# Ready steps by age with a credit for a bank, and attention masks as quarter products, in a planned four-layer transformer kernel

## The chip, the cores and the metric

The kernel runs on one core of one Trainium2 chip. The metric is the device time of one execution in microseconds, the median of three runs. A profile of one further execution, taken by the hardware profiler, stands beside it.

## The reference, cut to what matters

Four diffusion-transformer layers run one after the other over x of 16 x 256 x 256 (16 examples, 256 positions, width 256, 16 heads of 16), all in float32. The part that the change touches is the first layer's self-attention, which has a mask:

```python
def _attn(q, k, v, mask):
    scale = 1.0 / np.sqrt(HD)
    s = jnp.einsum('bqhd,bkhd->bhqk', q, k) * scale
    s = jnp.where(mask, s, jnp.finfo(s.dtype).min)
    a = jax.nn.softmax(s, axis=-1)
    return jnp.einsum('bhqk,bkhd->bqhd', a, v)
...
x_norm = _ln(x, norm1_w) * (1 + sc_msa) + sh_msa
q1, k1, v1 = qkv(x_norm[:, :n])
...
self_out = _attn(q, k, v, attn_mask[None, None]).reshape(b, s, d) @ attn_out_W
x = x + g_msa * self_out
xc = _ln(x, normc_w) * (1 + sc_x) + sh_x
...
cross = _attn(qc, kc, vc, cond_kv_mask[:, None, None, :]).reshape(b, s, d) @ co_W
x = x + g_x * cross
xm = _ln(x, norm2_w) * (1 + sc_mlp) + sh_mlp
h = jax.nn.gelu(xm @ mlp_W1 + mlp_b1, approximate=True)
return x + g_mlp * (h @ mlp_W2 + mlp_b2)
```

The mask of the self-attention is one table of 256 x 256 for all examples and heads. The second layer is a cross-attention alone (77 keys), the third has self-attention, cross-attention and an MLP without masks, and the fourth the same with rotated queries and keys.

## The kernel before, in words

**The work.** The activations stay in SBUF (`x_sb`). Six stretches follow each other: the attentions of layer 0 (names a for self, ac for cross), its MLP (b), the attentions of layers 1 and 2 (cx, c, cc), an MLP (d), those of layer 3 (e, ec), and the last MLP (f). Each attention of one example is a chain of steps: norm, projections (L591, L643, L763), first scores (L804 for self, L816 for cross) with queries along the partitions, from which VectorE takes each row's maximum (L830, L834, L838); these maxima go through DRAM into the extra rows of the queries; second scores (L898) with keys along the partitions, so that ScalarE's exponential (L912) gives what the product with the values needs (L921); a turn of the result on VectorE (L930), the reciprocal of the sums (L937, called the division here), the multiplication on GpSimd (L943), a turn back (L947), and the output projection with the residual (L968).

**Tiles of the array.** A head has 16 values, padded to a group of 32 rows of the array. Four groups of rows work side by side, each into its own bank of PSUM. A step of scores fills two banks (`rp` picks rows 0 and 32, or 64 and 96), and the planner puts two such steps together so that all four row groups are in use. The value products (L921) use four groups of columns in the same way.

**The mask in layer 0.** In the first scores of examples 0 and 1 (`by_pe`) the mask is a product with the identity in bf16 (L795), over the whole array, 512 columns into one bank; for the other 14 examples VectorE adds it while it takes the maximum (L830, one instruction and a short read-out for each half bank). In the second scores every bank gets its mask by such a product (L891): two products of the whole array for each step, ahead of the row-tiled scores L898, which add onto them. The masks `mb` and `mbT` (its transpose) are made at the start by `masks_in` and lie in a tile that a context buffer lends.

**What sets the order.** Nothing is scheduled by the hardware or a compiler here. The class `Order` collects all steps with an engine, an estimated duration, the steps they depend on and the buffers they take or use (`Hold`: PSUM banks "b", of which there are 8, and others such as `ts`, two, `oT`, two, `kq`, five). `solve` plays the steps through with those durations and so writes down one fixed order; each engine then executes its instructions in it. A buffer is given back when all its users are done. When an engine is free, `solve` sorts the steps that are ready (L178 to L179): on TensorE by priority, which rises with the example and the stage; on SP by `first`, then priority; on all other engines by `first`, then steps that hold a PSUM bank ahead of all others, then by the time at which they became ready. On ScalarE every step of the attentions and MLPs holds a bank, on GpSimd none does. On VectorE both kinds occur: reductions, L930, L616, the rotations (L655, L658) and the gated residuals hold one; the norm statistics (L466, L467), the division L937 and the turn back L947 don't. The estimate of a step of second scores is 2 x 0.432 us, and 0.48 more with a mask; that of a masked reduction is 0.95 us.

Of the kernel before, what the change touches and what calls it, by code (L numbers as in the profile page):

```python
# [16 lines left out]
B, N, D, H, HD, LC, FF = 16, 256, 256, 16, 16, 77, 1024  # L17
P = 128
NT = N // P
NC = D // P  # L20
NF = FF // P
CT = B * LC
# [51 lines left out]
class Order:  # L74
# [2 lines left out]
    LAG = 0.13  # L77
    TURN = {"row": 0.2, "col": 0.13}
    PATIENCE = 2.0
    PER_MB = 2.7  # L80
    FREE = ("b", "kq", "v")

# [20 lines left out]
    def solve(self):  # L103
# [66 lines left out]
        while n_done < len(self.tasks):  # L170
            progress = True
            while progress:
                progress = False
                for eng in list(waiting):
                    if eng != "NO" and free.get(eng, 0.0) > now + 1e-9:
                        continue
                    cand = [t for t in waiting[eng] if t.ready <= now + 1e-9]
                    cand.sort(key=lambda t: (t.prio, t.no) if eng == "PE" else (not t.first, t.prio, t.no) if eng == "SP" else  # L178
                              (not t.first, not any(h.tag == "b" for h in t.held), t.ready, t.prio, t.no))  # L179
                    cand = [t for t in cand if room(t)]  # L180
                    if cand:
                        ts = choose(cand) if eng == "PE" else [cand[0]]
                        if ts is not None:
                            begin(ts)
                            progress = True
            nxt = [e[0] for e in events[:1]]
            nxt += [t.ready for ts in waiting.values() for t in ts if t.ready > now + 1e-9]
            nxt += [t.since + self.PATIENCE for t in waiting.get("PE", ())
                    if t.since is not None and t.since + self.PATIENCE > now + 1e-9]
            assert nxt, "no step can start"  # L190
            now = min(nxt)
            while events and events[0][0] <= now + 1e-9:
                _, _, t = heapq.heappop(events)
                n_done += 1
                for h in t.held:
                    h.users -= 1
                    if not h.users and h.tag in loose:
                        loose[h.tag].append(h.no)
                    elif not h.users:
                        done_no[h.tag].add(h.no)  # L200
                        while ring[h.tag] in done_no[h.tag]:
                            done_no[h.tag].discard(ring[h.tag])
                            ring[h.tag] += 1
                for u in t.outs:
                    u.left -= 1
                    u.ready = max(u.ready, t.end + (self.LAG if u.eng != t.eng else 0.0))
                    if not u.left:
                        waiting.setdefault(u.eng, []).append(u)
# [4 lines left out]
def pixart_kernel(ctx: ExitStack, tc: tile.TileContext, x, cond_t, ctx_in, mask_c, mask_s, tables, vecs, rows,  # L213
                  mod0, mod1, mod2, mod3, wa, wb, wc, wd, we, wf, out):
    nc = tc.nc
    PSUM = bass.MemoryType.PSUM
    BF16 = mybir.dt.bfloat16
# [12 lines left out]
    ps = ctx.enter_context(tc.tile_pool(name="ps", bufs=1, space=PSUM))  # L230
# [3 lines left out]
    def psum(h, *dims):  # L234

        t = banks[h.no]
        return t.rearrange("p (a b) -> p a b", a=dims[0]) if dims else t
# [4 lines left out]
    identb = const.tile([P, P], BF16, name="identb")  # L242
# [14 lines left out]
    h_mask = Hold("ctx")  # L257
# [26 lines left out]
    add = od.add  # L284
    MM = 0.432
# [43 lines left out]
    t = add("PE", 0.4, rows_turn, take=[h_rt], prio=200)  # L329
# [360 lines left out]
    def attention(b, name, n, wv, wkeys, h_w, w_t, eps, mod, half, biases, masked, pre_add, gate, prio, ctxs=None,  # L690
# [177 lines left out]
        for g in range(NC):  # L868
            u5, h_av, h_so = {}, Hold("b"), Hold("ts")
            for kc in range(nk):  # L870
                h_e, ex = Hold("ec"), []

                def open_e(g=g, kc=kc):
                    if g == 0 and kc == 0:
                        s["oT"] = work.tile([P, NC, N], F32, tag="oT", bufs=CAPS["oT"], name=f"oT_{nm}")
                    for r in range(4):
                        s["e", g, kc, r] = work.tile([P, 2, N], F32, tag="e", bufs=4 * CAPS["ec"],
                                                     name=f"e_{nm}_{g}{kc}{r}")
                t_e = add("NO", 0.0, open_e, deps=[qx_t, v_t, barrier], take=[h_e] if g or kc else [h_e, h_ot],
                          prio=prio, line=("e", (nm, g, kc)))  # L880
                for rp in (1, 0):
                    hs = [Hold("b"), Hold("b")]
                    u = {}

                    def begin(g=g, kc=kc, rp=rp, u=u, hs=hs):
                        lists = []
                        for i in range(2):
                            r = 2 * rp + i
                            ps = u[i] = psum(hs[i])
                            if self_ and masked:  # L890
                                nc.tensor.matmul(ps.rearrange("p (s k) -> p s k", k=N), lhsT=identb,  # L891
                                                 rhs=mbT[:, kc, :].unsqueeze(1).to_broadcast([P, 2, N]),
                                                 start=True, stop=False)
                        for i in range(2):
                            r = 2 * rp + i
                            R = slice(32 * r, 32 * r + 32)
                            lists.append([
                                (lambda ps=u[i], R=R, q=q: nc.tensor.matmul(  # L898
                                    ps[0:rows_n, q * N:(q + 1) * N],
                                    lhsT=s["kz"][R, q, g, kc * P:kc * P + rows_n], rhs=s["qx"][R, q, g, :],  # L900
                                    start=not (self_ and masked), stop=not (self_ and masked) or q == 1))
                                for q in range(2)])
                        return lists
                    a = add("PE", 2 * MM, begin, more=0.48 if self_ and masked else 0.0,
                            deps=[t_e, k_t, *(mask_ts[self_][1] if masked else [])], take=hs, use=[h_kq, *h_masks], prio=prio, rp=rp, kind="e")
                    for i in range(2):
                        def exp(g=g, kc=kc, r=2 * rp + i, i=i, u=u):
                            e = s["e", g, kc, r][0:rows_n].rearrange("p s q -> p (s q)")
                            if masked and not self_:
                                nc.scalar.activation(e, u[i][0:rows_n], AF.Exp, bias=kbT[0:rows_n, b:b + 1])  # L910
                            else:
                                nc.scalar.activation(e, u[i][0:rows_n], AF.Exp)  # L912
                        ex.append(add("ACT", 0.6, exp, deps=[a], use=[hs[i], h_e], prio=prio))
                exps += ex

                def values(g=g, kc=kc, u5=u5, h_av=h_av):
                    if kc == 0:
                        u5["p"] = psum(h_av, 2)
                    for q in range(2):
                        for r in range(4):  # L920
                            nc.tensor.matmul(u5["p"][32 * r:32 * r + 32, 1 - q, :],  # L921
                                             lhsT=s["v"][0:rows_n, kc, 8 * g + 2 * r + 1 - q, :],
                                             rhs=s["e", g, kc, r][0:rows_n, q, :],
                                             start=(kc == 0 and q == 0), stop=(kc == nk - 1 and q == 1))
                a_av = add("PE", 2 * MM, values, deps=ex, take=[] if kc else [h_av],
                           use=[h_v, h_e] + ([h_av] if kc else []), prio=prio, kind="col", line=("av", (nm, g, kc)))
# [114 lines left out]

    mask_t = work.tile([P, NC, CT], F32, tag="ctxT", bufs=CAPS["ctx"], name="ctxT_masks")
    add("NO", 0.0, lambda: None, take=[h_mask], prio=-9)
    mask_b = mask_t.rearrange("p c n -> p (c n)")[:, 0:1152].bitcast(BF16)
    mb, mbT = (mask_b[:, i * 512:(i + 1) * 512].rearrange("p (t n) -> p t n", n=N) for i in range(2))
    junk = const.tile([P, N], F32, name="junk")
    kbm = mask_b[:, 1024:1024 + CT].rearrange("p (b n) -> p b n", n=LC)

    def load_x(b, prio, deps=()):
        def run():  # L1050
# [22 lines left out]
    def masks_in(prio):  # L1073
# [15 lines left out]

        def take():  # L1090
            nc.vector.tensor_copy(mbT, psum(hb, NT))
        t = add("SP", ISSUE, load, take=[hg], prio=prio, mb=0.07, lat=2.2)
        t = t1 = add("DVE", 1.2, floats, deps=[t], take=[ht], use=[hg, h_mask], prio=prio)
        t = add("PE", 4 * TR, turn, deps=[t], take=[hb], use=[ht], prio=prio)
        return t1, add("DVE", 0.5, take, deps=[t], use=[hb, h_mask], prio=prio)

    def key_masks_in(prio):
        u, hg, hb = {}, Hold("gb"), Hold("b")
# [244 lines left out]
```

## Time and profile before

| what | value |
|---|---|
| median of three runs | 2724.95 us (2724.75 to 2725.81) |
| the profiled execution, its own time | 2725.6 us |
| its span, first to last instruction | 2723.8 us |
| mean granted TensorE clock | 0.989 |
| TensorE busy | 2672.4 us (98%) |
| VectorE, ScalarE, GpSimd busy | 1543.9, 1238.8, 1064.8 us |
| chain that ended last | TensorE 92%, VectorE 3%, GpSimd 3% |
| masks of the second scores, L891 | 256 products, 376/379/634 ns (shortest, median, longest) |
| masked reductions, L830 | 448 at 423 ns, 189.4 us busy |

How to read it: PE is TensorE's products and PEld its loads of weights, DVE is VectorE, ACT ScalarE, POOL GpSimd, SP the engine that issues transfers. A matmul's end is modelled, and its recorded duration includes the way through the array, so products that follow each other overlap in the records: the distance of starts says what one costs. A busy TensorE is therefore not a TensorE at its peak, and the number of matmuls that pass in a stretch has to be compared. A product in fp32 stands in the trace as two matmuls. "Idle before, with a releaser" is how long an engine stood still before an instruction and what ended that.

### The profile page before, as it was taken

The page shows a single profiled execution, that of the slowest core. Times are in us where ns is not written, and L with a number is a line of the kernel's source. Part 1 is how long each engine was busy: PE and PEld are TensorE (multiplying, and loading weights), DVE is VectorE, ACT ScalarE, POOL GpSimd, SP SyncE. Part 2 cuts the span into 40 slices and gives each one's busy share as a digit, 9 for nine tenths or more (in the row PEclk, how much of TensorE's full clock was granted, in tenths as well). Part 3 has the DMA queues.
Part 4 walks back from the last instruction along what each step waited for, and adds up shares of the span by engine and source line. Part 5 has one row for each costly group of instructions (what it writes and reads, how often), then busy time and mean ns, then how long its engine had stood idle before and what let it go on. Part 6 is the DMA issues. An engine that isn't in the chain of part 4 may idle for free.

```text
span 2723.8 us, 55987 instructions
## 1 busy us (share of the span) xinstructions
PE 2672.4 (98%) x21888; PEld 1896.5 (70%) x21888; DVE 1543.9 (57%) x4377; ACT 1238.8 (45%) x2495; POOL 1064.8 (39%) x1413
## 2 busy tenths in 40 slices
PE   8999999999999999999999999999999999999999
PEld 5554555666888767666666676888766666666888
DVE  6787686566231267767776675110688876784110
ACT  2442444565332356555555554332445555554322
POOL 4322332455453435233334554433333323554321
PEclk9997999999999999999999999999999999999999
DMA  4000000011210010010000002000000000000000
GB/s 143 11 9 10 6 7 6 18 27 56 82 46 20 9 30 6 11 31 16 19 15 13 5 13 77 20 20 12 17 4 4 4 4 5 4 21 23 20 20 20
DMA packets 53569, 60.23 MB, mean 22 GB/s; under 512 B 19592, under 2 KB 38264, under 8 KB 52536
## 3 DMA queue, kind: packets, MB, share of 16 engines
q1 hardware_dynamic: 53304, 56.65, 7.1%
q8 instruction: 172, 2.82, 0.4%
q14 instruction: 93, 0.76, 0.1%
HBM read 50.44 MB, written 6.19 MB: 21 GB/s over the span
## 4 chain that ended last, share of the span: by engine, by line
PE 92%; DVE 3%; POOL 3%; issue 1%; ACT 1%; DMA 1%; DVEq 0%; POOLq 0%; ACTq 0%; SPq 0%
PE bank L968 19%; PE bank L898 13%; PE bank L1011 12%; PE bank L921 11%; PE bank L804 7%; PE bank L591 7%; PE bank L643 6%; PE bank L763 5%; PE bank L502 3%; PE bank L891 2%; PE bank L816 2%; PE bank L683 2%; DVE junk L830 1%; PE bank L387 1%; PE bank L578 0%
## 5 line engine op out<-in xcount | busy, mean ns | idle before, releaser
L898 PE MATMUL bank<-kq 32*128 32x256 f32 (+1 forms) x5120 | 596.6, 395 | 4.4 <-DMA kq<-mrow 3.6
L898 PEld LDWEIGHTS bank<-kq 32*128 32x128 f32 (+1 forms) x5120 | 349.3, 168 | 176.7 <-issue 120.5
L804 PE MATMUL bank<-kq 32*128 32x512 f32 x1536 | 408.9, 647 | 1.7 <-DVE kq L616 1.6
L912 ACT ACTIVATE e_a<-bank 128x512 f32<-128x512 f32 x256 | 136.8, 598 | 203.3 <-PE bank L804 120.6
L830 DVE CUSTOM_DVE_ANT_0 junk<-bank,ctxT_masks 128x256 f32<-128x256 f32 x448 | 189.4, 423 | 61.3 <-PE bank L804 28.9
L912 ACT ACTIVATE e_e<-bank 128x512 f32<-128x512 f32 x256 | 136.6, 599 | 145.4 <-PE bank L804 120.3
L834 DVE TENSOR_REDUCE mx_c<-bank 128x2 f32<-128x512 f32 x256 | 160.1, 682 | 36.5 <-PE bank L804 36.0
L834 DVE TENSOR_REDUCE mx_e<-bank 128x2 f32<-128x512 f32 x256 | 161.7, 683 | 31.2 <-PE bank L804 30.1
L912 ACT ACTIVATE e_c<-bank 128x512 f32<-128x512 f32 x256 | 134.6, 602 | 98.0 <-PE bank L804 70.1
L974 DVE TENSOR_TENSOR x_sb<-x_sb,bank 128x512 f32<-128x512 f32 x80 | 54.8, 684 | 210.4 <-PE bank L968 205.9
L816 PE MATMUL bank<-kq 32*128 32x154 f32 x2048 | 167.2, 309 | 0.2
L804 PEld LDWEIGHTS bank<-kq 32*128 32x128 f32 x1536 | 131.7, 186 | 37.4 <-DVE mx_a L830 11.5
L816 PEld LDWEIGHTS bank<-kq 32*128 32x128 f32 x2048 | 130.1, 185 | 14.9 <-issue 6.7
L1016 ACT ACTIVATE h_d<-bank,vec 128x256 f32<-128x256 f32 x128 | 53.7, 471 | 156.0 <-PE bank L1011 105.8
L1016 ACT ACTIVATE h_f<-bank,vec 128x256 f32<-128x256 f32 x128 | 53.7, 471 | 153.3 <-PE bank L1011 133.3
L1016 ACT ACTIVATE h_b<-bank,vec 128x256 f32<-128x256 f32 x128 | 53.6, 471 | 146.3 <-PE bank L1011 118.6
L1011 PE MATMUL bank<-xT_b,kq 128*128 128x256 f32 x512 | 113.8, 379 | 0.0
L1011 PE MATMUL bank<-xT_d,kq 128*128 128x256 f32 x512 | 113.6, 380 | 0.0
L1011 PE MATMUL bank<-xT_f,kq 128*128 128x256 f32 x512 | 113.3, 379 | 0.0
L968 PE MATMUL bank<-kq,h_b 128*128 128x256 f32 x512 | 113.2, 379 | 0.0
L968 PE MATMUL bank<-kq,h_d 128*128 128x256 f32 x512 | 113.2, 379 | 0.0
L968 PE MATMUL bank<-kq,h_f 128*128 128x256 f32 x512 | 113.2, 379 | 0.0
(335 smaller groups left out, 5777.2 us busy)
## 6 DMA issues: line engine op xcount, KB each, us to landing
kq<-in_mod_dram SPq DMA_DIRECT2D x10, 512.0 KB
cin<-in_ctx_in_dram SPq DMA_DIRECT2D x36, 128.0 KB
x_sb<-in_x_dram SPq DMA_DIRECT2D x16, 256.0 KB
gb_b<-gate_g0m SPq DMA_DIRECT2D x16, 256.0 KB
gb_c<-gate_g2a SPq DMA_DIRECT2D x16, 256.0 KB
gb_d<-gate_g2m SPq DMA_DIRECT2D x16, 256.0 KB
out_dram<-x_sb SPq DMA_DIRECT2D x16, 256.0 KB
kq<-mrow SPq DMA_DIRECT2D x224, 16.0 KB
```

The costliest lines, as they stand in the source:

```text
L591: nc.tensor.matmul(dst[:, g, :], lhsT=w[:, k, g * P:(g + 1) * P], rhs=xT[:, k, :], start=(k == 0), stop=(k == NC - 1))
L643: nc.tensor.matmul(u["p"][0:r, at:at + D], lhsT=xT()[:, k, t * P:t * P + r], rhs=w()[:, k, :], start=(k == 0), stop=(k == NC - 1))
L804: ls.append(lambda ps=ps, R=R, keys=keys: nc.tensor.matmul(ps.rearrange("p (s k) -> p s k", k=N), lhsT=s["qx"][R, 0, g, t * P:(t + 1) * P] ...
L816: ls.append(lambda ps=ps, R=R, keys=keys, tt=tt: nc.tensor.matmul(ps[:, 2 * tt * n:2 * (tt + 1) * n].rearrange("p (s k) -> p s k", k=n), l ...
L830: nc.vector.tensor_tensor_reduce(junk, u[i][:, i2 * N:(i2 + 1) * N], mb[:, t, :], -1.0, 3.0e38, ALU.add, ALU.min, m[:, i2, g, t:t + 1])
L834: nc.vector.tensor_reduce(m[:, :, g, t], u[i].rearrange("p (s k) -> p s k", k=N), AX.X, ALU.max, negate=True)
L898: (lambda ps=u[i], R=R, q=q: nc.tensor.matmul(ps[0:rows_n, q * N:(q + 1) * N], lhsT=s["kz"][R, q, g, kc * P:kc * P + rows_n], rhs=s["qx"][ ...
L912: nc.scalar.activation(e, u[i][0:rows_n], AF.Exp)
L921: nc.tensor.matmul(u5["p"][32 * r:32 * r + 32, 1 - q, :], lhsT=s["v"][0:rows_n, kc, 8 * g + 2 * r + 1 - q, :], rhs=s["e", g, kc, r][0:rows ...
L968: nc.tensor.matmul(u["p"][:, t, :], lhsT=lhsT(k, t), rhs=w()[:, k, :], start=(k == 0), stop=(k == nk - 1))
L1011: nc.tensor.matmul(u["p"][:, j, :], lhsT=wv["w1"][:, k, f * P:(f + 1) * P], rhs=s["xT"][:, k, :], start=(k == 0), stop=(k == NC - 1))
L1016: nc.scalar.activation(s["h", i][:, j, :], u["p"][:, j, :], func, bias=vcol(b1, 2 * i + j))
```

## The change

Two edits.

In the planner, the sort key of VectorE, ScalarE and GpSimd no longer puts every step that holds a bank first. Steps are taken by the time at which they became ready, and one that holds a bank counts as 3.0 us (`FAVOUR`) older than it is.

In the second scores of layer 0 the mask of a bank is no longer one product of the whole array. Each bank's product is cut in two halves of keys, 64 rows and 64 columns of the identity, and a step's four quarters are arranged so that they use the four quarters of the array: bank 0 takes keys 0 to 63 by rows 0 to 63 and keys 64 to 127 by rows 64 to 127; bank 1 takes keys 0 to 63 by rows 64 to 127 and keys 64 to 127 by rows 0 to 63. For bank 1 the mask therefore has to lie with its two halves of partitions swapped: `mbR`, a third tile of masks, is made at the start by two more copies out of PSUM. The planner's cost of the masks goes from 0.48 to 0.26 us a step, that of the step that makes the masks from 0.5 to 1.4.

```diff
+    FAVOUR = 3.0
...
-                              (not t.first, not any(h.tag == "b" for h in t.held), t.ready, t.prio, t.no))
+                              (not t.first, t.ready - self.FAVOUR * any(h.tag == "b" for h in t.held), t.prio, t.no))
...
-                            ps = u[i] = psum(hs[i])
-                            if self_ and masked:
-                                nc.tensor.matmul(ps.rearrange("p (s k) -> p s k", k=N), lhsT=identb,
-                                                 rhs=mbT[:, kc, :].unsqueeze(1).to_broadcast([P, 2, N]),
+                            u[i] = psum(hs[i])
+                        for j in range(2):
+                            for i in range(2 if self_ and masked else 0):
+
+                                K, M = slice(64 * (i ^ j), 64 * (i ^ j) + 64), slice(64 * j, 64 * j + 64)
+                                nc.tensor.matmul(u[i][M].rearrange("p (s k) -> p s k", k=N), lhsT=identb[K, K],
+                                                 rhs=(mbR if i else mbT)[K, kc, :].unsqueeze(1).to_broadcast([64, 2, N]),
                                                  start=True, stop=False)
...
-                    a = add("PE", 2 * MM, begin, more=0.48 if self_ and masked else 0.0,
+                    a = add("PE", 2 * MM, begin, more=0.26 if self_ and masked else 0.0,
...
-    mask_b = mask_t.rearrange("p c n -> p (c n)")[:, 0:1152].bitcast(BF16)
+    mask_b = mask_t.rearrange("p c n -> p (c n)")[:, 0:1408].bitcast(BF16)
...
-    kbm = mask_b[:, 1024:1024 + CT].rearrange("p (b n) -> p b n", n=LC)
+    mbR = mask_b[:, 1024:1536].rearrange("p (t n) -> p t n", n=N)
+    kbm = mask_b[:, 1536:1536 + CT].rearrange("p (b n) -> p b n", n=LC)
...
             nc.vector.tensor_copy(mbT, psum(hb, NT))
+            for i in range(2):
+                nc.vector.tensor_copy(mbR[64 - 64 * i:P - 64 * i], psum(hb, NT)[64 * i:64 * i + 64])
...
-        return t1, add("DVE", 0.5, take, deps=[t], use=[hb, h_mask], prio=prio)
+        return t1, add("DVE", 1.4, take, deps=[t], use=[hb, h_mask], prio=prio)
```

## The prediction

> **What bounds the kernel now.** I read the page's busy shares first, then the busy time by stretches of 50 us, then the waits and the timeline of the stretch that stood out, last the mask product's own records. TensorE is the bound:
>
> ```profile
> PE 2672.4 (98%) x21888; PEld 1896.5 (70%) x21888; DVE 1543.9 (57%) x4377; ACT 1238.8 (45%) x2495; POOL 1064.8 (39%) x1413
> ```
>
> So a gain is had only where TensorE works less or where its "busy" is hollow. Busy time by stretch (columns: stretch, length, then busy us and instructions of PE, PEld, DVE, ACT, POOL, then granted clock, DMA share, GB/s), layer 0's self-attention:
>
> ```profile
> 150.00:200.00 50.00, 50.00 (x411) 28.54 (x409) 42.12 (x174) 21.18 (x39) 13.15 (x16) 1.00 0.04 9
> 200.00:250.00 50.00, 48.68 (x251) 24.99 (x252) 43.30 (x193) 10.28 (x20) 6.68 (x8) 0.79 0.03 7
> 250.00:300.00 50.00, 45.20 (x367) 24.97 (x368) 23.30 (x86) 20.52 (x40) 16.76 (x23) 0.87 0.04 10
> 350.00:400.00 50.00, 50.00 (x423) 29.66 (x425) 40.42 (x161) 21.39 (x40) 17.39 (x22) 1.00 0.03 9
> ```
>
> All four claim a nearly full TensorE, yet 200 to 300 passes 618 matmuls where its neighbours pass about 418 per 50 us, 836 per 100: 218 are missing, 26 us at their rate, and the clock falls to 0.79. The timeline there (start, duration, what, idle before):
>
> ```profile
> 230.97 21.18 PE L804 MATMUL bank<-kq 32*128 32x512 f32 x44
> ...
> 257.50 0.23 DVE L937 RECIPROCAL rec_a<-ts_a 128x8 f32<-128x8 f32 x2
> ...
> 257.74 0.76 POOL L943 TENSOR_TENSOR od_a<-ts_a,rec_a 128x128 f32<-128x128 f32 x2 [28.50 <-DVE rec_a L937]
> 257.97 0.67 DVE L930 STREAM_TRANSPOSE ts_a<-bank 128x512 f32<-128x512 f32 x1
> 258.10 2.92 PE L968 MATMUL bank<-w_a,oT_a 128*128 128x256 f32 x6 [4.79 <-DVE oT_a L947]
> ```
>
> The turn L930 before this one stood at 214.5 (0.67 us); its division L937 starts at 257.50, 42 us late. It holds no bank, so on VectorE every ready reduction (L830) was put before it. Undivided tiles keep both `ts` buffers, so the next turn (257.97), the residual (258.10) and new second scores wait too. TensorE is left with first scores alone, one bank per reduction: 44 passes, 22 banks, in 21.2 us.
>
> **What the Trainium skill says.** "TensorE: Matmul & The Clock Gate", Part 3: products on different tiles of the array run together, "MM_dur + (ntile−1)×4ns". The trace agrees for rows and for columns apart: L898's records on other rows start 6 to 7 ns apart, so do L921's on other columns, and the next round 209 to 216 ns later; rows and columns at once, as in the change, it doesn't show. "TensorEngine Tiling (Array Packing)": by its Key Properties a change of tiling mode drains the array, by its Restrictions column tiling switches the fast weight load off. The drain is in the trace: mask product to scores takes 309 ns, mask product to mask product 216 to 226, so 93 ns (309 - 216) a change. Its Gotcha 1 says that row tiles cannot write one bank at the same time; "PSUM — Partial Sum Buffer", on bank collisions, puts the limit at bank and quadrant, and the quarters of one bank lie in other quadrants. Nothing in the trace settles this.
>
> **The change, part by part.** The sum is made against the profiled execution, 2725.6 us (span 2723.8, 1.8 around it); the median of the runs is 2724.95, 0.65 below, which I take off at the end.
>
> ```profile
> L891 PEld LDWEIGHTS <-identb x256: 95/98/151, 53.2 to 501.0; 128*128 128x128 bf16 x128
> L891 PE MATMUL bank<-ctxT_masks,identb x256: 376/379/634, 53.4 to 501.2; 128*128 128x512 bf16 x128
> ```
> ```profile
> 340.21 0.60 PE L891 MATMUL bank<-ctxT_masks,identb 128*128 128x512 bf16 x2
> 340.74 0.19 PEld L898 LDWEIGHTS bank<-kq 32*128 32x128 f32 x2 [0.42 <-issue]
> ```
>
> (1) Masks by quarters. A step of two banks now takes 0.535 us from its first mask product to its scores (226 + 309 ns; above, 340.21 to 340.74). There are 256 products in 128 steps. After: four quarters, 512 columns each. If they run together: one product of 216 ns, three starts 7 ns apart (21), the drain of 93, and a load that nothing hides. A first load of 128 fp32 columns lengthens its product by 104 ns (478 against 374), of 32 columns by 24 (403 against 379): 0.8 ns a column, so some 52 ns for 64 columns without the fast load. Sum 0.382, saved 0.153. Where two such steps stand together the second pair's loads hide, saved about 0.19 a step. I take 0.16: 128 x 0.16 = **-20.5 us**. Best end: a whole product saved, 128 x 0.216 = -27.6. Worst end: all four one after another, (4 x 226 - 2 x 226) x 128 = +58. TensorE is the bound here, so the saving is on the path as far as VectorE follows, term (4).
>
> (2) More changes of mode. In the order of the instructions, layer 0 passes 465 changes of tiling before and 518 after: mask products on the whole array could follow projections without one, quarters cannot. 53 x 0.093 = **+5 us**.
>
> (3) Age in place of banks first. In VectorE's order the most instructions between a turn L930 and its division falls from 163 to 30, the longest run of reductions from 64 to 32. After the opening, where no second scores exist yet, TensorE's longest run of first scores in layer 0 falls from 36 to 10. So this stall goes. Its size: the 22 banks alone took 21.2 us; in a full group (340.74 to 341.81) four banks take 1.07, so 22 take 5.9: 15.3 lost. The wait before L968 5, the waits for the rotated queries before 231 some 5, half clock on the way out some 3: 28, and 26 by the counted matmuls. I take **-28 us** (25 to 31). TensorE's groups are as many in both orders (layer 0: 197 and 196; last attention: 194 and 194); in the middle one 259 became 262, 3 x 1.0 = **+3 us**, between 0 and 5. ScalarE's steps all hold banks and GpSimd's none, so their rule stays in effect; SP's and TensorE's are untouched. Outside layer 0 the new rule only moves VectorE steps within slack: from 950 to 1650 VectorE is busy 481 of 700 us, from 1915 to 2480 442 of 565.
>
> (4) What is late next: VectorE. Never idle, it reads 43.3 of 50 (200 to 250), 0.87. From 50 to 500 it is busy 322.8, so it needs 371 us. TensorE would leave 450 - 28 - 20.5 = 402: VectorE at 92%. From 150 to 200 it ran at 42.1/43.3 = 97% with TensorE undisturbed, but the order is fixed from costs that put a masked reduction at 0.95 where the trace has 1.04 (241.76 to 242.80), so it will come late and hold banks. I give **+10 us**, from 0 to 16.
>
> (5) Two more copies of half a mask tile (L1097, L1098 of the new file), at most 0.74 each by L616's row for a whole tile, before the first L891 at 53 us; VectorE is busy 36 of the first 50 us, which hides them: 0, or +1.5 without that cover. Nothing is added to a queue of DMAs.
>
> Sum: -20.5 + 5 - 28 + 3 + 10 = **-30.5 us**: 2695.1 on the profiled scale, **2694** on the median's. Its own range: low ends -27.6 + 5 - 31 + 0 + 0 = -54, high ends -19.5 + 5 - 25 + 3 + 16 = -20: 2671 to 2705.
>
> **The rivals.**
> *VectorE takes the place of the bound.* Half of what TensorE is given back, (28 + 20.5)/2, is lost to banks that come late: -24 + 5 + 3 = -16, 2709. For it: the 92% above, and the waits for `mx_a` before L804. Against it: 97% without harm.
> *The quarters don't do what they say*: the pair on one bank runs after the pair before it. Two rounds cost as much as now plus the bare load (53 - 10) x 128 = +5.5; VectorE is then pressed less (+5): -28 + 5.5 + 5 + 3 + 5 = -9.5, 2715. For it: Gotcha 1. Against it: the quadrants differ.
> *Slower*: the quarters run one by one, loads included. +58 - 28 + 5 + 3 = +38, 2763. It decides from the point where a step of four quarters takes over 0.7 us to its scores, since 128 x (0.7 - 0.535) = 21 eats what the order's terms leave (28 - 5 - 3). For it: no product of this trace uses part of the rows and part of the columns. Against it: rows and columns each run together.
>
> **Numbers.** Forecast 0.60, VectorE 0.20, two rounds 0.12, one by one 0.08. The range reaches from the forecast's low end to the two rounds: 2671 to 2715, about 0.8 of the cases. A measurement of this kernel can tell some 0.2%, 5.4 us: the first three are faster by more, except a part of the two rounds and of VectorE's case (0.05), so faster 0.87, within 0.05, slower 0.08.
>
> **What would show it.** In the changed profile: 512 quarter products whose starts lie under 60 ns apart within a step, and some 0.38 us from the first to the scores (0.54: two rounds; over 0.7: one by one). No stretch of layer 0 with a clock of 0.8, the first MLP's products beginning some 34 us earlier, none of it from later layers; GpSimd's longest wait for L937 in layer 0 far below 28.5 us. VectorE at or above 41 of 50 us there; if waits of L804 and L898's loads for reductions grow beyond 10 us, VectorE's rival holds. Wrong would be a new stall of the same kind in a later attention, or a step's gain that VectorE eats whole.

## The result, and the profile after

The changed kernel takes 2685.03 us (median of four runs, 2683.71 to 2687.25), the kernel before 2724.85: a ratio of 0.9856, 95% interval 0.9838 to 0.9873. The forecast was 2694 with a range of 2671 to 2715, so the time lies inside, 9 us below the forecast.

The page of the changed kernel, busy times:

```profile
PE 2635.8 (98%) x22144; PEld 1887.2 (70%) x22144; DVE 1542.2 (57%) x4379; ACT 1240.1 (46%) x2495; POOL 1065.7 (40%) x1413
```

TensorE is as full as before with 37 us less in it. Busy time by stretches of 50 us (stretch, length, PE, PEld, DVE, ACT, POOL, granted clock, DMA share, GB/s), the same place in layer 0 as before:

```profile
150.00:200.00 50.00, 49.78 (x472) 29.12 (x474) 41.43 (x169) 23.03 (x43) 17.34 (x22) 1.00 0.03 9
200.00:250.00 50.00, 50.00 (x480) 31.17 (x468) 41.81 (x172) 23.93 (x46) 17.30 (x22) 1.00 0.04 9
250.00:300.00 50.00, 49.78 (x468) 29.12 (x464) 41.33 (x170) 22.59 (x42) 17.34 (x22) 1.00 0.03 9
```

These stretches now pass some 470 matmuls each, part of them short quarters, at the full clock; the hole of 251 at 0.79 is gone, and VectorE is at 41 to 42 of 50. The longest time from a turn to the division of its result in layer 0 (L934 to L941 in the changed kernel's numbering, L930 to L937 before) fell from 43.0 to 7.8 us, and GpSimd's longest wait for a division from 28.5 to 13.7. The quarter products, by their records and in the timeline:

```profile
L895 PEld LDWEIGHTS <-identb x512: 102/103/106, 54.5 to 457.8; 64*64 64x64 bf16 x171
L895 PE MATMUL bank<-ctxT_masks,identb x512: 372/400/400, 54.5 to 458.0; 64*64 64x512 bf16 x171
```
```profile
340.79 0.41 PE L895 MATMUL bank<-ctxT_masks,identb 64*64 64x512 bf16 x4
341.13 0.19 PEld L902 LDWEIGHTS bank<-kq 32*128 32x128 f32 x2 [0.23 <-issue]
```

The four stand in one line because they start 3 to 4 ns apart; 0.34 us later the scores begin, where two whole products took 0.535. The last mask product stands at 458.0, before at 501.2.

Where the time went, by the start of the first product of each stretch (us of the span, from the records of the two profiles):

```
                     before   after
layer 0 attentions    683.2   641.9   -41.3
first MLP             239.1   239.0
layers 1, 2           761.6   760.7    -0.9
second MLP            232.0   232.0
last attentions       575.0   576.0    +1.0
last MLP              233.0   233.1
```

The whole gain is in layer 0's attentions.

### The profile page after: what moved, and what is told of

Read it like the earlier page. It is cut to its first block, busy times and chain, and to the rows that moved or that the text cites. A ratio compares the mean times of both kernels' runs of the same rounds, so it can differ in the third digit from the quotient of the medians.

```text
span 2682.7 us, 56475 instructions
## 1 busy us (share of the span) xinstructions
PE 2635.8 (98%) x22144; PEld 1887.2 (70%) x22144; DVE 1542.2 (57%) x4379; ACT 1240.1 (46%) x2495; POOL 1065.7 (40%) x1413
## 4 chain that ended last, share of the span: by engine, by line
PE 92%; DVE 3%; POOL 2%; ACT 1%; issue 1%; DMA 1%; DVEq 0%; ACTq 0%; POOLq 0%; SPq 0%
PE bank L972 20%; PE bank L902 13%; PE bank L1015 12%; PE bank L925 11%; PE bank L805 7%; PE bank L592 7%; PE bank L644 6%; PE bank L764 5%; PE bank L503 3%; PE bank L817 2%; PE bank L684 2%; PE bank L895 2%; PE bank L388 1%; PE bank L579 0%; ACT e_ac L914 0%
## 5 line engine op out<-in xcount | busy, mean ns | idle before, releaser
L902 PE MATMUL bank<-kq 32*128 32x256 f32 (+1 forms) x5120 | 606.2, 396 | 2.9 <-DMA kq<-mrow 2.5
L902 PEld LDWEIGHTS bank<-kq 32*128 32x128 f32 (+1 forms) x5120 | 354.3, 168 | 158.4 <-issue 108.2
L805 PE MATMUL bank<-kq 32*128 32x512 f32 x1536 | 411.1, 638 | 1.9 <-DVE kq L617 1.8
L805 PEld LDWEIGHTS bank<-kq 32*128 32x128 f32 x1536 | 127.4, 184 | 25.2 <-issue 8.1
```

What stands on the lines that cost most here:

```text
L805: ls.append(lambda ps=ps, R=R, keys=keys: nc.tensor.matmul(ps.rearrange("p (s k) -> p s k", k=N), lhsT=s["qx"][R, 0, g, t * P:(t + 1) * P] ...
L902: (lambda ps=u[i], R=R, q=q: nc.tensor.matmul(ps[0:rows_n, q * N:(q + 1) * N], lhsT=s["kz"][R, q, g, kc * P:kc * P + rows_n], rhs=s["qx"][ ...
```

## The experiments

Each was timed in four to six runs beside the kernel before, and a bracket after a ratio is its 95% interval; "layer 0" is the first stretch of the table above in the run's own profile. The kernel before had medians of 2724.8 to 2726.9 beside them. Two profiles of one layer 0 order differ by up to 3.7 us (the changed kernel and favour_e0), so single layer 0 lengths are not read finer than that. Medians are compared with the changed kernel's 2685.03, which was measured at another time; differences of some 2 us, the range of the kernel before, are not read.

**masks_only**: the quarters with the old sort key.

```diff
-  (not t.first, t.ready - self.FAVOUR * any(h.tag == "b" for h in t.held), t.prio, t.no))
+  (not t.first, not any(h.tag == "b" for h in t.held), t.ready, t.prio, t.no))
```

> The quarter products with the sort key of before (banks first). Theory that two separate gains add up (masks about 25 us, since a step falls from 0.535 to 0.340 us 128 times; order the rest): about 2700 us, with a stall of the old kind (first scores alone, a division L937 that comes tens of us late) still in layer 0. Rival, VectorE takes the place of the bound without the new order: the steps are as short, but the stalls grow and the time stays above 2712 us.

Measured 2738.53 us, ratio 1.0051 (1.0039 to 1.0063): slower than before; layer 0 694.1. The steps are as short as in the changed kernel (0.340 us). The stretches and the timeline of this run:

```profile
150.00:200.00 50.00, 49.83 (x357) 23.25 (x350) 42.36 (x186) 14.63 (x26) 3.74 (x3) 0.90 0.04 10
...
400.00:450.00 50.00, 44.09 (x278) 22.53 (x280) 33.31 (x134) 11.35 (x21) 8.09 (x12) 0.73 0.03 8
```
```profile
400.43 22.31 PE L805 MATMUL bank<-kq 32*128 32x512 f32 x44 [0.39 <-DVE mx_a L831]
...
427.51 1.22 PE L972 MATMUL bank<-w_a,oT_a 128*128 128x256 f32 x2 [4.77 <-DVE oT_a L951]
```

Two stalls of the old kind, where one stood: 44 passes of first scores alone from 400, and 36 in 17.8 us from 184. The sum of two separate gains, some 2700, is refuted; the rival's numbers hold, but not its reason, as the next run shows.

**plan_before_quarters**: is it the short steps or the plan? The kernel before with its own order and quarters issued in it.

```diff
+  # masks_only, with the costs of before
-  more=0.26 if self_ and masked else 0.0
+  more=0.48 if self_ and masked else 0.0
-  return t1, add("DVE", 1.4, take, ...
+  return t1, add("DVE", 0.5, take, ...
```

> The kernel before with its own order, unchanged on every engine (masks planned at 0.48), and only the mask products cut into quarters, with the two copies for the swapped mask. Theory that masks_only is slow because the lower planned cost led the banks-first rule into other and longer stalls: here the gain of the masks is had, 10 to 19 us outside the old stall, 2707 to 2716 us. Rival, that shorter steps themselves starve VectorE's other steps whatever the plan: 2725 us or above.

Measured 2712.18 us, ratio 0.9950 (0.9937 to 0.9964), layer 0 670.1. The quarters by themselves gain 13 us in the old order, with the old stall in it:

```profile
226.47 21.91 PE L805 MATMUL bank<-kq 32*128 32x512 f32 x44
...
253.74 0.23 DVE L941 RECIPROCAL rec_a<-ts_a 128x8 f32<-128x8 f32 x2
```

The stall begins 4.5 us earlier than before and is as long. So masks_only loses by the order that banks-first draws from the changed costs, not by the products. Two costs differ between these runs, that of a step of second scores and that of making the masks; which of them drew the stalls wasn't tested.

**order_only**: the new key with the whole-array products and the old costs.

```diff
+    FAVOUR = 3.0
-  (not t.first, not any(h.tag == "b" for h in t.held), t.ready, t.prio, t.no))
+  (not t.first, t.ready - self.FAVOUR * any(h.tag == "b" for h in t.held), t.prio, t.no))
```

> The sort key by age with a credit of 3.0 us, with the whole-array mask products and their cost of before. Theory that the gains add: 2724.9 - 16 to -28, so 2697 to 2709 us, no stall with a clock of 0.8. Rival, that the stall's end only moves the wait elsewhere and the masks make the whole gain: above 2718 us.

Measured 2712.4 us (2704.8 to 2719.07), ratio 0.9950 (0.9938 to 0.9963), layer 0 667.8. The stretch from 200 to 250 is whole:

```profile
200.00:250.00 50.00, 50.00 (x438) 29.13 (x432) 40.33 (x164) 23.47 (x44) 16.66 (x23) 1.00 0.04 8
```

A gain by the key alone, with the stall gone, but smaller than the 16 to 28 us expected; the rival, that the masks make the whole gain, is refuted too.

**plan_after_full** and **same_quarters**: the changed kernel's order with other mask products.

```diff
-  for j in range(2): ... lhsT=identb[K, K], rhs=(mbR if i else mbT)[K, kc, :] ...
+  nc.tensor.matmul(u[i] ..., lhsT=identb, rhs=mbT[:, kc, :] ...)            # plan_after_full
+  K = M = slice(64 * j, 64 * j + 64), rhs=mbT[K, kc, :] for both banks      # same_quarters
```

> The changed kernel's plan, every engine's other instructions in the same order, but each bank's mask by one product of the whole array as before. Theory that TensorE is the bound in layer 0: 128 steps at 0.195 us more each, 25 us over the changed kernel, 2710 us. Rival, VectorE is the bound there after the change: TensorE's additional 25 us lie beside VectorE's work in part, 2690 to 2700 us.

> The changed kernel with both banks' quarters on the same two quarters of the array (keys 0 to 63 on rows and columns 0 to 63 for both banks, 64 to 127 on rows and columns 64 to 127), the same sums and the same order. Theory that it is the four different quarters that make a step short: two rounds, some 0.34 + 0.22 = 0.556 us a step, 128 x 0.216 = 27 us over the changed kernel, 2712 us. Rival, that it is the halved size alone: a step stays near 0.34 us and the time at 2685 us.

plan_after_full: 2703.81 us, ratio 0.9915 (0.9902 to 0.9928), layer 0 660.9: 19 us over the changed kernel, and between the two expectations. It divides the gain with the plan held fixed: the order as planned in the change brings 22 us of layer 0 (683.2 to 660.9), the quarters 19 (660.9 to 641.9).

That 19 is less than 25 is TensorE's own doing. A whole product follows a projection without a change of tiling, a quarter doesn't. The same place in plan_after_full and in the changed kernel, eight matmuls of a projection and then the masks:

```profile
161.86 1.99 PE L644 MATMUL bank<-w_a,xT_a 128*128 128x256 f32 x8
163.69 0.59 PE L892 MATMUL bank<-ctxT_masks,identb 128*128 128x512 bf16 x2
```
```profile
158.76 1.99 PE L644 MATMUL bank<-w_a,xT_a 128*128 128x256 f32 x8
160.69 0.41 PE L895 MATMUL bank<-ctxT_masks,identb 64*64 64x512 bf16 x4
```

From the last matmul of the projection to the mask product it is 216 ns in the first and 309 in the second, so 93 more. By the records this comes 46 times in the 128 steps, 4 us, which the 25 don't count. TensorE has some 20 us less to do, and 19 of them are time.

same_quarters: 2708.5 us, ratio 0.9940 (0.9928 to 0.9951), 23 us over, against 27 expected. A step:

```profile
301.07 0.62 PE L895 MATMUL bank<-ctxT_masks,identb 64*64 64x512 bf16 x4
301.62 0.19 PEld L902 LDWEIGHTS bank<-kq 32*128 32x128 f32 x2 [0.41 <-issue]
```

0.55 us: two rounds, some 233 ns apart. The records don't name the quarter, so which two ran together isn't shown. Shown is that the halved size alone doesn't make a step short: the four have to lie on different quarters.

**favour0** and **favour12**: other credits.

```diff
-    FAVOUR = 3.0
+    FAVOUR = 0.0      # favour0
+    FAVOUR = 12.0     # favour12
```

> The changed kernel with a credit of 0: pure age. Theory that the end of banks first is what counts and the credit hardly: within 6 us of the changed kernel, 2680 to 2691 us, divisions on time. Rival, that without a credit reductions wait behind steps that hold no bank and TensorE waits for banks: over 2695 us.

> The changed kernel with a credit of 12 us, on the way back to banks first (most instructions between a turn and its division 66 by the order, 30 with a credit of 3, 163 before). Theory that late divisions make the stalls: 2690 to 2705 us, with GpSimd waits for the division above 15 us. Rival, that only the extreme of banks first stalls: 2685 us.

favour0: 2692.18 us, ratio 0.9877 (0.9863 to 0.9890), between the two expectations. Layer 0 is as long as in the changed kernel (641.9); layers 1 and 2 take 774.3 in place of 760.7 and the last attentions 569.1 in place of 576.0. The credit counts in the middle, then, and costs at the end. favour12: 2700.14 us, ratio 0.9907 (0.9894 to 0.9921), layer 0 651.7. The time was as expected, the sign for it not: GpSimd's longest wait for a division is 13.7 us as in the changed kernel. A smaller hole of the old kind is there all the same, with half the clock for 10 of its us:

```profile
200.00:250.00 50.00, 45.40 (x346) 26.00 (x340) 41.16 (x174) 16.09 (x30) 15.18 (x19) 0.90 0.04 8
230.23 2.93 PE L972 MATMUL bank<-w_a,oT_a 128*128 128x256 f32 x6 [3.42 <-DVE oT_a L951]
```

TensorE waits there for a turn back, which holds no bank either. Divisions come up to 15.6 us after their turn (7.8 in the changed kernel), and the waits of self-attention for its norm statistics grow, while those of cross-attention (`rstd_ac`) fall from 32.8 to 10.2 us. What each of these is worth of the 15 us, of which 10 are in layer 0, isn't shown. Of the waits from 50 to 500 us (waiter, awaited, total, times, longest), the changed kernel and then favour12:

```profile
POOL od_a L947 <- DVE rec_a L941: 68.2, 15, 13.7
POOL rstd_a L473 <- DVE mv_a L468: 36.2, 11, 7.6
```
```profile
POOL rstd_a L473 <- DVE mv_a L468: 58.2, 9, 22.6
POOL od_a L947 <- DVE rec_a L941: 43.9, 12, 13.7
```

**dve_cost**, **half_reduce**, **by_pe1**: what VectorE costs after the change.

```diff
-  add("DVE", 0.95 if self_ and masked and not by_pe ...
+  add("DVE", 1.04 if self_ and masked and not by_pe ...                               # dve_cost
-  junk, u[i][:, i2 * N:(i2 + 1) * N], mb[:, t, :], ...
+  junk[:, 0:P], u[i][:, i2 * N + P:(i2 + 1) * N], mb[:, t, P:N], ...                  # half_reduce
-    BY_PE = 2
+    BY_PE = 1                                                                         # by_pe1
```

> The changed kernel with a masked reduction planned at 1.04 us, as the trace has it, in place of 0.95. Theory that VectorE, planned too light, comes late and holds banks after the change: 3 to 8 us less, 2677 to 2682 us. Rival, that TensorE is the bound and lateness doesn't matter: 2685 us within 3.

> The changed kernel with the masked maxima over keys 128 to 255 alone; keys 0 to 127 are left out of the maxima, the order on every engine stays. Takes some 0.1 us from each of 448 reductions, 50 to 60 us from VectorE in layer 0. Theory that VectorE's lateness still costs TensorE time there: 4 to 10 us less than the changed kernel, 2675 to 2681 us. Rival, that TensorE alone is the bound of layer 0 now: 2685 us within 3.

> The changed kernel with one example's first-score masks on TensorE in place of two: 16 fewer whole-array products (16 x 0.226 = 3.6 us, and some changes of tiling) for TensorE, 32 masked half reductions, about 5 us, more for VectorE. Theory that both are near their limit in layer 0: within 3 us of 2685 us. Rival, TensorE alone is the bound: 2680 us or less.

dve_cost: 2686.26 us, ratio 0.9857 (0.9843 to 0.9870): nothing gained by a truer cost, the rival's value. half_reduce: 2680.16 us, ratio 0.9833 (0.9820 to 0.9846), layer 0 637.5. VectorE's busy time from 50 to 450 falls from 317.0 to 264.2:

```profile
50.00:450.00 400.00, 396.20 (x3748) 239.80 (x3745) 316.99 (x1246) 183.97 (x347) 128.75 (x164) 1.00 0.04 11
```
```profile
50.00:450.00 400.00, 396.44 (x3802) 240.57 (x3800) 264.21 (x1250) 187.49 (x354) 128.47 (x164) 1.00 0.04 11
```

With 53 us taken from VectorE the kernel gains 5, 4.4 of them in layer 0, hardly more than the 3.7 by which two profiles of one order differ. The size is as the theory had it; at most VectorE costs TensorE a little in layer 0, and it isn't its bound. by_pe1: 2691.39 us, ratio 0.9877 (0.9864 to 0.9891), layer 0 648.9: 6 us slower where both theories had less. VectorE's additional 5 us alone are not an explanation by what half_reduce shows; the order drawn is another one too, and the cause stays open.

**favour_e0** and **first_quarters**: a better kernel.

```diff
+  t.ready - self.FAVOUR * (t.prio < 1120) * any(h.tag == "b" for h in t.held)         # favour_e0
+  # first_quarters: favour_e0, and L796's products of examples 0 and 1 as four quarters,
+  # with mbS, the swapped copy of mb
```

> The changed kernel with the credit set to 0 from the last layer's attentions on, 3.0 before them. Theory that what the credit costs or brings is settled stretch by stretch by the order drawn there, and that the 6.9 us which a credit of 0 saved in the last attention are had without its loss in the middle ones: 2678 us. Rival, that they came from the state in which the stretch before left the engines: 2685 us.

> The kernel of favour_e0 with the 32 mask products of the first scores of examples 0 and 1 as quarters too, the order of all else unchanged, two more copies at the start. Theory that a step's shortening is time where VectorE has slack, as it has with these two examples (their maxima take no masks): 16 steps at 0.1 to 0.2 us, 2 to 3 us less than favour_e0, so 2677 us. Rival, that the copies ahead of the first scores or waits for banks eat it: 2680 us.

favour_e0: 2679.83 us, ratio 0.9833 (0.9819 to 0.9846); the last attentions take 568.8 us, so the 7 us of favour0 are had where they arose. first_quarters: 2676.73 us (2673.79 to 2684.2), ratio 0.9825 (0.9812 to 0.9838): the median is as expected, but its interval overlaps most of that of favour_e0, so a gain over favour_e0 isn't shown. Its interval touches that of the changed kernel (0.9838 to 0.9873) only at the end.

## Why the prediction was right, and where its terms were off

**(1) Masks, -20.5.** Right in mechanism: four quarters at once, a load laid bare, one change of tiling behind them. The size was off in one term: the load of 64 columns lengthens its product by 21 ns (400 against the 379 of the whole product), not by 52, and the starts lie 3 to 4 ns apart. A step takes 216 + 10 + 93 + 21 = 340 ns, so 0.195 us is saved, 128 x 0.195 = 25 of TensorE's time. The two rounds of the rival stand in same_quarters, at 23 us; the changed kernel doesn't have them, and the slower rival, one by one, is excluded by the same records.

**(2) More changes of tiling, +5.** Right in mechanism and size: 46 steps pay 93 ns ahead of their quarters, 4 us. It is a cost of the quarters and not of the order, since plan_after_full, in the same order, doesn't have it. (1) and (2) together were -15.5; measured with the plan held fixed they are -19. In the old order the quarters brought only 13 (plan_before_quarters): the stall there stayed as long as it was, and where the rest went isn't shown.

**(3) Order, -28, and (4) VectorE, +10.** The stall goes, as order_only, plan_after_full and the changed kernel show. Together the two terms were -18; measured, from the kernel before to plan_after_full, -22. How much of the difference is the order's and how much VectorE's isn't separated. +10 for VectorE was probably too high: the loads of the first and second scores (L805, L902) wait 2.3 us for reductions in layer 0, where those of the kernel before waited 13.2, so the sign that the prediction set for VectorE's rival (growing beyond 10) isn't there; half_reduce gains 5 by a lighter VectorE; and the reason given, that its cost is planned too low, fell with dve_cost. It runs at 41 to 42 of 50, as forecast.

**Do the parts add up?** With the plan held fixed they do: -22 by the order and -19 by the quarters make the -41 of layer 0. Across plans they don't: 2725 becomes 2712 by the quarters in the old order, 2712 by the new key alone, 2739 by the quarters with their costs under the old key, and 2685 by all. The prediction had read its counts from the order that the change really draws, and so had priced that plan; its sum holds for that plan and says nothing of the key in others.

**Groups, +3 in the middle attentions.** Wrong by 3: those stretches moved by -0.9, and the other profiles with the same sequence of products there (order_only, plan_after_full, same_quarters, half_reduce, favour_e0, first_quarters) have 761.5 to 763.2 against 761.6 before. Three more groups in the order were no time that can be seen. The last attentions moved by +1.0.

**(5) The two copies** at the start: the first mask product stands at 54.5 us, before at 53.4, and the stretch from 50 to 100 has TensorE busy throughout (50.00). No more than that 1.1 us.

Together, on the profiled scale: -41.1 us in the span against -30.5. The difference of 10.6 is masks and changes of tiling 3.5, order and VectorE 4, groups 3. All three were off in the same direction, so the forecast did not come near by errors that cancel.

## What to carry to other kernels

In a plan with fixed orders, a rule that always serves the holders of the scarcest buffer can starve the steps that give other buffers back, as here the division, 43 us after its turn. Age with a small credit avoided it here, and the sign was a late step that holds nothing scarce, not a busy engine. The credit is no constant: of 0, 3 and 12 us the 3 was best over the whole, and 0 was better in the last attentions. A change of costs redraws such a plan: test a faster step with the order kept, and with the order redrawn, before it is judged, since here the same quarters were worth -13, +14 or, beside the new rule, -19 us. A product with a matrix that is zero outside its diagonal blocks, as the identity is, can leave the zero blocks out: here four blocks of 64 x 64 on different rows and columns took one round (340 ns a step), where two whole products took 535. Count the changes of tiling that this adds.

## What the runs showed of the hardware

The row-and-column quarters ran together although two row groups wrote one bank at a time, in other partitions of it: 340 ns a step. That decides, for this pattern, between the two pages of the Trainium skill that the prediction had set side by side: "PSUM — Partial Sum Buffer" with its limit by bank and quadrant agrees, Gotcha 1 of "TensorEngine Tiling (Array Packing)", taken by whole banks, doesn't. What two row groups do in one quadrant of a bank no run here shows.

A load of 64 bf16 columns was nearly hidden (21 ns), cheaper than the trace's fp32 loads by column (0.8 ns, so 52) had led to expect. And going from projections on the whole array to 64 x 64 quarters costs 93 ns between starts (309 in place of 216), as much as the change from whole mask products to scores in the kernel before.
